# Four gated cross-attention layers on one core: L3's routing moved into the attention before it, half of L2's folding moved into L1's mixture

## The chip, the cores and the metric

The kernel runs on one core of a Trainium2 chip. The core has five engines with instruction streams of their own: TensorE (PE: matmuls and transposes, from SBUF into PSUM), VectorE (DVE), ScalarE (ACT: activation functions through loaded tables, copies), GpSimd (POOL: here mostly powers, some elementwise work, and the issuing of indirect DMAs) and SyncE (SP: issues the other DMAs). They wait for one another through semaphores. The metric is the device time of one execution in microseconds (us); a smaller number is better. All data are float32.

## The reference

The state `x` has 8 sequences of 256 tokens with 128 features (2048 tokens); the context `ctx_2048` has 8 x 64 tokens of 256 features. Four layers, L0 to L3, each add a cross attention and a feed-forward part, both behind a layer norm and scaled by a tanh gate:

```python
for n in range(4):
    x = x + tanh(g_xattn[n]) * Ln_xattn(layernorm(x), ctx_2048, ...)
    x = x + tanh(g_ffn[n])   * Ln_ffn(layernorm(x), ...)
```

The parts are, cut to what matters here:

- `L0_ffn`: a base SwiGLU MLP and the top 2 of 8 SwiGLU experts.
- `L1_xattn`: 16 heads of 8 features; the keys are the layer's own 256 tokens and the 64 context tokens.
- `L1_ffn`: the top 2 of 8 gelu experts (hidden size 64) and a shared expert:

```python
scores = sigmoid(x @ gate_W) * route_scale          # 8 experts
gate_full = top-2 of scores, divided by their sum, zero elsewhere
h = gelu(einsum('bsd,edh->bseh', x, W1) + b1)
out = sum_e gate_full[e] * (h[e] @ W2[e] + b2[e]) + gelu(x @ Ws1 + bs1) @ Ws2 + bs2
```

- `L2_xattn`: 16 heads of 64, keys and values from the context plus one null key and value; the output is layer-normed.

```python
q = x @ Wq;  k, v = split(context @ Wkv)            # 16 heads of 64
k = concat(null_k, k);  v = concat(null_v, v)
out = layernorm(softmax(q k^T / 8) v @ Wout) * ln_scale + ln_bias
```

- `L2_ffn`: an attention whose projections are mixed over 8 experts, and then 8 gelu experts.
- `L3_xattn`: 8 heads of 16 over the masked context tokens, without projections.
- `L3_ffn`: a shared silu expert, and the one expert of 8 with the largest router probability, both with weights quantised to three values a row:

```python
h = layernorm(x) * ln_gamma + ln_beta
probs = softmax(h @ router_w.T)                     # 8 experts
out = shared(h) + max(probs) * expert[argmax(probs)](h)
```

## The kernel before

**Tiling.** `x` stays in SBUF as 16 tiles of 128 tokens. A chunk (`c`, 0 to 3) is 512 tokens, four tiles; a half is two chunks, eight tiles (`HT`). Two large SBUF tiles, `arena_a` and `arena_b`, hold one layer's weights and intermediates after another's; a new use of an arena waits for the old one's readers. PSUM is handed out in banks of 128x512 (`bank`) and pairs of banks (`banks2`). The steps run in the order `l0, l1_xattn, l1_ffn, l2_xattn, l2_ffn, l3_xattn, l3_ffn`.

**What sets the order.** In L0 to L2 a tile scheduler places each engine's instructions from the order of the program and the dependences; `behind(X)` keeps what is issued in it behind instruction X. A tile of a pool may be given memory that another pool's closed tile had; its first writer then waits for that tile's last readers. In L3 (`manual_schedule`) each engine issues in the order of the program.

**L0's end and L1's attention.** L0's feed-forward gathers rows of expert results back to their tokens with indirect DMAs (`gather`, L610) through the index tile `dp_rows`, made in `placed` (L585). L1's attention goes over the eight sequences `bb`: `maxima(bb)` forms scores (`sc`, L983) and their negated maxima (`nmx`, L992); `finish()` turns the maxima with PE (`pm`, L999), copies them (`nmT`, L1001) and sends them by DMA into four rows of the queries (L1003), so that `outputs(bb)` can form exponentials of scores less maximum (`stc` L1022, `st` L1038, `pT` L1047) and sum values (`o`, L1064), divide, turn and project. `prepare(c)` makes chunk c's queries, keys and values ahead, in pieces (`extra`) set among the steps.

**L1's mixture** (`l1_ffn`): `route(0)`, `route(1)` (norm, turn `pt` L272, copy `xT` L1150, logits `lg` L1152, sigmoid L1156, top 2 into `w4`), then `hidden(c)` (five matmuls `ph` L1168 and gelus L1175, L1178) one chunk ahead of `output(c)`: turn the weights (`pg`, `gt` L1188), spread them over hidden rows (`pgb`, L1193), multiply on DVE, and contract (`yt` L1197, L1198, L1200), turn back and add to x. Issue order:

```python
route(0)
route(1)
hg = hidden(0)
for c in range(NCH):
    nxt = hidden(c + 1) if c + 1 < NCH else None
    output(c, hg)
    hg = nxt
```

**L2's folding** (in `l2_xattn`): for each k of 8 pairs of heads, keys and values of the context are formed (`pk` L1374, `pv` L1379) and multiplied into Wq and Wout (`pg` L1395, `pu` L1407), which gives `G` and `U`; scores of L2's attention are then x times G. The null key and value give `gn` (L1363) and `nvu` (L1365). POOL clears `nkb` and two block-diagonal tiles `vds` by memset.

**L3.** `l3_xattn` runs 16 tiles through a software pipeline with a step for each tile; `beside(t, f, ...)` sets work for L3's feed-forward at the end of steps t, t+1, and so on. That is `normed3(c)` (normed x for the attention's queries), `logits3(c)` (stats, norm with z written to DRAM, turn and router logits L1968) and `routed3(half)` (largest logit, counts, positions, and the index list `idx` by which tiles of 128 tokens with one expert each are gathered: 8 + 7 = 15 tiles a half). `l3_ffn` gathers these tiles (`fetched3`: `xr` from z, on POOL, L610), and loops over 30 tiles: `turn`, `first` (L2031, silu), `turn_back` (L2039), `second` (`yr`, L2048, written to DRAM as y). `wide`, `shared`, `back` (L2063, L2070, L2078) are the shared expert of a chunk; `combined(half)` gathers y back by token and adds it. The tail is the gathering for half 1 and the write of the output.

Of the kernel before, what the change touches and what calls it, by code (L numbers as in the profile page):

```python
# [24 lines left out]
P = 128  # L25
# [3 lines left out]
NCH = 4  # L29
# [8 lines left out]
def tile_flamingo(ctx: ExitStack, tc: tile.TileContext, a: dict, out: bass.AP, n_sub: int = 8):  # L38
# [9 lines left out]
    @contextmanager  # L48
    def psum(singles, pairs):

        with ExitStack() as st:
            for n, bufs in ((1, singles), (2, pairs)):
                if not bufs:
                    continue
                ps[n] = st.enter_context(tc.tile_pool(name=f"ps{n}", bufs=bufs, space=bass.MemoryType.PSUM))
            yield
# [458 lines left out]
    def counted(pool, masks):  # L515
# [10 lines left out]
        v.tensor_copy(cnt, pc)  # L526
        return cnt

    def placed(pool, masks, cnt, consts):
# [55 lines left out]
        rows = mk(pool, [P, n_sel, HT], "dp_rows", dtype=I32)  # L585
# [369 lines left out]
    def l1_xattn():  # L955
# [5 lines left out]
        with psum(2, 3), tc.tile_pool(name="l1x", bufs=2) as lp:  # L961
# [140 lines left out]
            before, after = None, []  # L1102
            for bb in range(B):
# [3 lines left out]
                extra = prepare(ahead) if bb % BPC == 0 and ahead < NCH else []  # L1107
                for n in range(5):
# [8 lines left out]
                    for q in (extra, after):  # L1117
                        if q and (q is extra or n > 0):
                            q.pop(0)()
# [9 lines left out]
            before(3)  # L1129
            for f in after:  # L1130
                f()


    def l1_ffn():
        load2()
        with psum(8, 0), tc.tile_pool(name="l1f", bufs=2) as lp:

            e_pair = mk(lp, [P, 4, P], "e_pair", bufs=1)
            for j in range(4):
                r = slice(32 * j, 32 * j + E)  # L1140
                v.tensor_copy(e_pair[r].rearrange("p g (t h) -> p (g t) h", t=2), over(ident[r, r], 64))
            w4 = mk(lp, [P, NT, 4, 32], "w4", bufs=1)
            g.memset(w4, 0.0)
            xT = mk(lp, [P, NCH, CW], "xT", bufs=1)

            def route(half):
                lg = bank([P, HT, E], "lg")
                for k2 in range(2):
                    c = 2 * half + k2
                    s.copy(xT[:, c, :], transposed(layernorm(c)))  # L1150
                    for k in range(TPC):
                        pe.matmul(  # L1152
                            lg[:, k2 * TPC + k, :], xT[:, c, k * P : (k + 1) * P], gw1, start=True, stop=True
                        )
                sc = mk(rt, [P, HT, E], "sm_p")
                s.activation(sc, lg, AF.Sigmoid)  # L1156
# [1039 lines left out]
```

## Time and profile before

| | us |
|---|---|
| median of 3 timed runs (lowest to highest) | 1296.32 (1294.29 to 1307.2) |
| profiled execution, its own time | 1218.13 |
| its span, mean granted clock | 1216.3, 0.909 |
| PE busy, share of span | 1043.9, 86% |
| DVE, ACT, POOL busy | 640.1, 442.5, 304.9 |
| L1's attention, from its first scores to the last values | 231 to 491 |
| L1's mixture | 491 to 576 |
| L2's folding | 576 to 639.5 |
| L2's attention and feed-forward | 639.5 to 1056 |
| L3's attention | 1056 to 1129 |
| L3's feed-forward up to the last `yr` | 1129 to 1198 |
| tail | 1198 to 1216.3 |

The stages are read from the timeline's times, and overlap a little. Times on the page are from the span's start. The "granted clock" is the share of full speed that the throttle gave PE. A line of the timeline has start, length, engine, line, operation and operands, and, in brackets, the engine's idle time just before it and what ended it. The chain of waits is followed back from the last instruction, at each step to what released it.

### The profile page before, as it was taken

Reading aid. Unit: us, or ns where it says so; the run is one execution under the profiler, and the core shown is the slowest. Engines: PE = TensorE matmul, PEld = TensorE weight load, DVE = VectorE, ACT = ScalarE, POOL = GpSimd, SP = SyncE. Lnnn points to the kernel's source line nnn. Section 1 sums busy time; section 2 is a strip of 40 time slices with the busy share of each in tenths; the row PEclk is TensorE's granted clock in tenths of the full one; section 3 lists DMA queues with packets and bytes.
Section 4 is the critical chain, followed back from the end, with each engine's and each line's share of the span. In section 5 each row is a group of like instructions: output and inputs, shape, how many; then the busy total and the mean of one; then the engine's idle time right before and its main releaser. Section 6 shows DMA issues by size and latency. Waiting matters only on the chain.

```text
span 1216.3 us, 15651 instructions
## 1 busy us (share of the span) xinstructions
PE 1043.9 (86%) x5570; PEld 580.8 (48%) x5570; DVE 640.1 (53%) x1776; ACT 442.5 (36%) x860; POOL 304.9 (25%) x341
## 2 busy tenths in 40 slices
PE   5889998848999899898998987879998989875894
PEld 4548756624444444533555654334433333343573
DVE  4574536535555454534237996454463733487353
ACT  3623433313344345422234444122102443364442
POOL 2137541221000000101102555122231410132554
PEclk9889999858999999788898997889989999997798
DMA  9203310200000012300000000200000000000233
GB/s 241 68 20 57 76 46 19 58 24 20 3 20 2 19 42 65 104 0 1 1 1 1 1 1 9 78 1 0 1 1 1 0 1 1 0 10 9 50 70 98
DMA packets 50811, 37.04 MB, mean 30 GB/s; under 512 B 10280, under 2 KB 46672, under 8 KB 50480
## 3 DMA queue, kind: packets, MB, share of 16 engines
q1 hardware_dynamic: 45488, 26.83, 8.0%
q0 software_dynamic: 3968, 8.13, 3.7%
q10 hardware_dynamic: 1280, 1.09, 0.5%
q8 instruction: 45, 0.74, 0.3%
q14 instruction: 30, 0.25, 0.1%
HBM read 25.34 MB, written 8.13 MB: 28 GB/s over the span
## 4 chain that ended last, share of the span: by engine, by line
PE 65%; DVE 16%; ACT 6%; issue 5%; POOL 5%; DMA 1%; SPq 0%; POOLq 0%; DVEq 0%; ACTq 0%
PE pymT L1610 5%; PE st L1038 4%; PE gur L768 3%; PE o L1064 3%; PE pqmT L1610 3%; DVE nmx L992 3%; PE sc L983 3%; PE phm L1693 2%; PE pgb L1591 2%; PE pvmT L1610 2%; PE pkmT L1610 2%; PE yr L793 2%; PE yt L1200 2%; PE gu L744 2%; POOL xn L610 1%
## 5 line engine op out<-in xcount | busy, mean ns | idle before, releaser
L992 DVE TENSOR_REDUCE nmx<-sc 128x2 f32<-128x640 f32 x128 | 97.5, 818 | 64.1 <-PE sc L983 63.0
L221 POOL TENSOR_TENSOR rstd<-rstd,mhalf 128x4 f32<-128x4 f32 (+1 forms) x36 | 34.2, 949 | 343.3 <-DVE rstd L236 296.4
L1047 ACT ACTIVATE pT<-st 128x1024 f32<-128x1024 f32 x64 | 62.1, 1021 | 104.6 <-PE st L1038 104.6
L768 PE MATMUL gur<-arena_a,xrT 128*128 x184 | 63.6, 471 | 0.4
L1610 PE MATMUL pymT<-xe,arena_b 128*128 128x512 f32 x128 | 61.7, 638 | 2.6 <-DVE xe L1602 2.6
L610 POOL DMA_INDIRECT xr<-xk,dp_src x46 | 46.8, 1017 | 43.3 <-DVE lg_m L289 29.7
L1464 POOL TENSOR_TENSOR arena_a<-arena_a,rs 128x1024 f32<-128x1024 f32 x16 | 30.4, 1901 | 92.6 <-DVE rs L1463 77.9
L1591 PE MATMUL pgb<-gt,e_sel 8*128 8x512 f32 x192 | 40.4, 704 | 7.6 <-ACT gt L1584 7.6
L983 PE MATMUL sc<-arena_b 29*128 29x320 f32 x256 | 41.1, 553 | 4.7 <-DVE nmx L992 4.0
L785 DVE COPY aTr<-pta 128x256 f32<-128x256 f32 x46 | 19.5, 424 | 47.6 <-PE pta L783 47.5
L1610 PEld LDWEIGHTS pymT<-xe,arena_b 128*128 128x128 f32 x128 | 25.4, 204 | 38.6 <-issue 23.7
L610 POOL DMA_INDIRECT xn<-yg,dp_rows x32 | 30.4, 950 | 41.9 <-issue 32.1
L983 PE MATMUL sc<-arena_a 29*128 29x320 f32 x256 | 35.8, 472 | 4.2 <-DVE nmx L992 3.9
L277 DVE SCALAR_TENSOR_TENSOR x<-yt,tg,x 128x512 f32<-128x512 f32 x16 | 11.9, 748 | 51.5 <-PE yt L1205 25.7
L768 PEld LDWEIGHTS gur<-arena_a,xrT 128*128 128x128 f32 x184 | 32.2, 193 | 13.5 <-issue 2.1
L793 PE MATMUL yr<-arena_a,aTr 128*128 (+1 forms) x276 | 38.3, 276 | 0.0
L1443 PE MATMUL sc<-G,t2k 128*128 128x512 f32 x64 | 34.3, 633 | 4.6 <-DVE rs L1462 3.7
L1940 POOL TENSOR_TENSOR arena_a<-arena_a 128x256 f32<-128x256 f32 x18 | 13.6, 757 | 91.0 <-DVE arena_a L1939 90.5
L610 POOL DMA_INDIRECT xr<-z,dp_src x30 | 28.5, 951 | 30.0 <-DVE rstd L1953 14.7
L776 ACT ACTIVATE sgr<-gur 128x352 f32<-128x352 f32 x46 | 21.4, 465 | 39.5 <-PE gur L768 39.5
L1038 PE MATMUL st<-arena_b 32*128 32x256 f32 x256 | 34.6, 466 | 1.3 <-DVE nmx L992 1.0
L1610 PE MATMUL pqmT<-xe,arena_b 128*128 128x512 f32 x64 | 35.1, 711 | 0.0
(505 smaller groups left out, 2400.6 us busy)
## 6 DMA issues: line engine op xcount, KB each, us to landing
arena_a<-in_L_ffn_exp_wgu_dram SPq DMA_DIRECT2D x2, 1408.0 KB
yg<-yr SPq DMA_DIRECT2D x10, 256.0 KB
arena_a<-in_L_xattn_Wkv_dram SPq DMA_DIRECT2D x1, 2048.0 KB
y<-yr SPq DMA_DIRECT2D x6, 256.0 KB
x<-in_x_dram SPq DMA_DIRECT2D x4, 256.0 KB
arena_b<-in_ctx_dram ACTq DMA_DIRECT2D x2, 512.0 KB
arena_a<-in_L_ffn_exp_wd_dram SPq DMA_DIRECT2D x2, 512.0 KB
xk<-xk SPq DMA_DIRECT2D x4, 256.0 KB
```

The costliest lines, as they stand in the source:

```text
L221: g.tensor_tensor(dst, src, mhalf[:, 0:n], ALU.pow)
L610: return g.indirect_dma_start(out=dst, out_offset=None, in_=src, in_offset=bass.IndirectOffsetOnAxis(ap=idx, axis=0))
L768: pe.matmul(gu[:, h, 0:352], xrT[t], wgu[:, bass.ds(e + 1, 1), h * 352 : h * 352 + 352].rearrange("p e f -> p (e f)"), start=True, stop=True,)
L793: pe.matmul(y, aT[0:n, i, :], wd[0:n, bass.ds(e + 1, 1), i, :].rearrange("p e d -> p (e d)"), start=(i == 0), stop=(i == 2),)
L983: pe.matmul(scs[j // 2][:, j % 2, 0:K], qp[i : i + 29, k4, t], kp[i : i + 29, k4, b, :], start=True, stop=True,)
L992: l1["max"] = v.tensor_reduce(nmx[qt][:, h0 : h0 + 2], scs[pr][:, :, 0:K], AX.X, ALU.max, negate=True)
L1038: pe.matmul(sts[j // 2][:, j % 2, kt, :], kp[i : i + 32, k4, b, kt * P : (kt + 1) * P], qp[i : i + 32, k4, tb], start=True, stop=True,)
L1047: s.activation(pT[k4, pr], sts[pr], AF.Exp)
L1064: pe.matmul(o[kk][32 * i : 32 * i + n, k, :], w, e, start=(step == 0), stop=(step == 2))
L1443: pe.matmul(sc[:, 8 * k : 8 * k + 8, :].rearrange("p h m -> p (h m)"), xT[:, q], G[:, b, 8 * k : 8 * k + 8, :].rearrange("p h m -> p (h m) ...
L1591: pe.matmul(pg, e_sel4[r, e, :], gt[r], start=True, stop=True)
L1610: pe.matmul(pq, w[:, e, :], xe[:, e, :], start=(e == 0), stop=(e == E - 1))
```

## The change

The change has three groups; the words that came with it name the second and third.

1. `placed` takes the tile `dp_rows` from the constant pool, with two buffers for each count of selections, instead of from the pool of the step that calls it. It serves L0 and L3.
2. `l1_ffn` and `l2_xattn` become one step, `l1_l2`, in one PSUM layout. Chunk 0's norm and logits (`route1(0)`), and the expander `e_pair`, are set into the last two sequences of L1's attention, and `hidden1(0)` before its last divide. Sigmoid becomes 1/(1+exp(-x)) on raw logits. Four of the eight foldings of L2 are placed among the outputs of the mixture; the null key and value, L2's constants and the load of L2's feed-forward weights (`load2`) come behind it. `w4` and `vds` are cleared by ACT copies instead of POOL memsets; the spread weights are multiplied in pairs of banks. Pieces of `prepare` are put behind the latest maximum. `G` and `U` become two tiles each.
3. In L3's attention the steps that prepare the feed-forward come a step earlier, the turn and the logits are steps of their own, half 0's whole routing lies in steps 11 to 15 and its gathers begin at step 15. The exponential and the probability of the routed expert (`weighed3`) are taken out of the routing. In L3's feed-forward the expert tiles come first; logits of chunks 2 and 3, routing of half 1 and the shared expert of chunks 0 to 2 lie among them.

```diff
@@ placed @@
-        rows = mk(pool, [P, n_sel, HT], "dp_rows", dtype=I32)
+        rows = mk(const, [P, n_sel, HT], f"dp_rows{n_sel}", bufs=2, dtype=I32)
...
@@ l1_xattn @@
-        with psum(2, 3), tc.tile_pool(name="l1x", bufs=2) as lp:
+        with psum(2, 3, True), tc.tile_pool(name="l1x", bufs=2) as lp:
...
+            asides = {6: [lambda: None, l1_arena], 7: route1(0, misc)}
...
-                extra = prepare(ahead) if bb % BPC == 0 and ahead < NCH else []
+                extra = prepare(ahead) if bb % BPC == 0 and ahead < NCH else asides.get(bb, [])
...
-                            q.pop(0)()
+                            with behind(l1["max"]) if q is extra else ExitStack():
+                                q.pop(0)()
...
             before(3)
+            hidden1(0, l1["hg0"])
             for f in after:
                 f()
...
@@ l1_ffn @@
-            w4 = mk(lp, [P, NT, 4, 32], "w4", bufs=1)
-            g.memset(w4, 0.0)
+        w4 = mk(lp, [P, NT, 4, 32], "w4", bufs=1)
+        clear(w4.rearrange("p n j e -> p (n j e)"))
...
-                s.activation(sc, lg, AF.Sigmoid)
-                v.tensor_scalar(sc, sc, rscale, None, ALU.mult)
+            s.activation(sc, es[:, h, :], AF.Exp, scale=-1.0)
+            v.tensor_scalar(sc, sc, 1.0, None, ALU.add)
+            v.reciprocal(sc, sc)
+            v.tensor_scalar(sc, sc, rscale, None, ALU.mult)
...
+        steps = [route1(c, misc) for c in range(1, NCH)]
+        for norm, logits in steps[:1]:
+            norm()
+            logits()
+        hidden(1)
+        for norm, logits in steps[1:]:
+            norm()
+            logits()
+        routed(0)
+        hidden(2)
+        fold()
+        with behind(l1["ph"]):
+            output(0)
+        fold()
+        routed(1)
+        hidden(3)
+        output(1)
+        fold()
+        output(2)
+        fold()
+        output(3)
+        fold()
...
@@ l2_xattn, now in l1_l2 @@
-            for t in vds:
-                g.memset(t, 0.0)
...
+            def folds():
...
+                with behind(l1["ph"]):
+                    kv = keys_values(0)
+                yield
                 for k in range(8):
+                    nxt = keys_values(k + 1) if k < 7 else None
+                    fold(k, *kv)
+                    kv = nxt
+                    yield
...
+            for t in vds:
+                for b4 in range(2):
+                    clear(t[:, 4 * b4 : 4 * b4 + 4].rearrange("p b t m -> p (b t m)"))
+            pieces = folds()
+            with tc.tile_pool(name="l1f", bufs=2) as lp:
+                l1_ffn(lp, misc, lambda: next(pieces))
+            late_tiles(r2["pool"], 0)
+            load2()
+            with tc.tile_pool(name="l2c", bufs=1) as cp, tc.tile_pool(name="l2x", bufs=2) as lp:
+                half_tiles(cp)
+                constants2()
+                run_all(pieces)
+                l2_xattn(lp)
...
@@ l3_xattn @@
-            beside(3, *normed3(2))
-            beside(7, *normed3(3))
+            beside(2, *normed3(2))
+            beside(6, *normed3(3))
             for c in range(2):
-                beside(4 * c + 5, *logits3(c))
+                beside(4 * c + 4, *logits3(c))
             steps = routed3(0)
-            beside(12, *[lambda: next(steps, None)] * 5)
-            beside(13, *logits3(2))
+            beside(11, *[lambda: next(steps, None)] * 5)
+            n_tiles = HT + E - 1
+            beside(15, lambda: fetched3(0, range(4)))
+            q3["late"] = logits3(2), logits3(3)
+            beside(15, *q3["late"][0][0:2])
+            beside(16, lambda: (q3["late"][1][0](), fetched3(0, range(4, n_tiles))))
...
@@ logits3, routed3 @@
-        return [stats, norm, logits]
+        return [stats, norm, turn, logits]
...
-        s.activation(pr, pr, AF.Exp)
...
+    def weighed3(half):
+
+        pr = q3["pr", half]
+        s.activation(pr, pr, AF.Exp)
+        q3["w", half] = w = mk(q3["pool"], [P, HT], "w3")
+        row_sum(w, pr)
+        v.reciprocal(w, w)
+        v.tensor_scalar(w, w, tg[:, 7:8], None, ALU.mult)
...
@@ l3_ffn @@
+            weighed3(0)
+            turn2, logits2 = q3["late"][0][2:]
+            norm3, turn3, logits3_ = q3["late"][1][1:]
+            norm3()
+            turn2()
+            beside(-2, logits2, turn3, logits3_)
+            beside(1, *[lambda: next(steps, None)] * 5)
+            aside[6] = [lambda: fetched3(1, range(n_tiles))]
...
+            for i in range(3):
+                shared_beside(7 + 3 * i, i)
+            aside[n_tiles].append(lambda: backs.extend(combined(0)))
...
+            weighed3(1)
             h3 = wide(3)
             tail = combined(1)
             y3 = shared(3, h3)
+            backs[0]()
+            backs[1]()
             back(3, y3)
```

`clear(dst)` is an ACT copy of zeros, used before in L1's preparation; `shared_beside(t, c)` sets `wide(c)`, `shared(c)` and `back(c)` at tiles t, t+1 and t+2.

## The prediction

> **What bounds the kernel now.** I read the page first, to see which engine carries the end; then the table of windows, cut at the stages, to see where that engine is not working at full speed; then the timeline and the chain of waits inside the stages that the diff touches.
>
> ```profile
> PEclk9889999858999999788898997889989999997798
> PE 65%; DVE 16%; ACT 6%; issue 5%; POOL 5%; DMA 1%; SPq 0%; POOLq 0%; DVEq 0%; ACTq 0%
> ```
>
> The second line is the chain that ended last: TensorE (PE) has 65% of it. The first is the granted clock in 40 slices of 30.4 us, in tenths: it is not full in most. So what can be won is time in which PE waits, and PE work done at less than full clock. The columns of the next lines are window, its length, busy us and instructions of PE, PE weight loads, VectorE (DVE), ScalarE (ACT) and GpSimd (POOL), then PE clock, DMA share and GB/s.
>
> ```profile
> 490.00:523.00 33.00, 27.58 (x112) 16.55 (x104) 18.35 (x68) 15.54 (x23) 4.92 (x5) 0.74 0.30 96
> 523.00:582.00 59.00, 51.01 (x129) 19.26 (x128) 21.85 (x73) 13.91 (x21) 7.93 (x7) 0.86 0.00 0
> 582.00:640.00 58.00, 56.46 (x256) 33.48 (x257) 18.08 (x32) 18.57 (x33) 0.00 (x0) 0.94 0.00 1
> 1070.00:1125.00 55.00, 36.12 (x180) 20.88 (x178) 43.03 (x136) 29.57 (x65) 16.77 (x17) 0.82 0.03 10
> 1125.00:1170.00 45.00, 38.98 (x192) 28.51 (x193) 19.57 (x77) 20.55 (x45) 23.02 (x25) 0.80 0.27 55
> 1170.00:1200.00 30.00, 28.90 (x187) 23.36 (x185) 16.36 (x48) 15.66 (x40) 14.11 (x15) 1.00 0.49 103
> ```
>
> L1's mixture (490 to 582) and the start of L2's folding run at clock 0.74 to 0.94, with PE idle for 15 of the first 150 us. L3's attention (1070 to 1125) has PE busy 36 of 55 us; the start of L3's FFN (1125 to 1170) has clock 0.80.
>
> **Part C, the rows tile (not in the change's words).** `dp_rows` moves from L0's pool to the constant pool. In the timeline:
>
> ```profile
> 244.21 0.38 PE L999 MATMUL pm<-ident,nmx 128*16 128x128 f32 x1
> 256.62 0.41 DVE L1001 COPY nmT<-pm 16x256 f32<-16x256 f32 x1 [11.47 <-DMA xn<-yg,dp_rows]
> ```
>
> The first copy `nmT` of L1's attention has its input at 244.6, but waits until 256.6 for the last gathers of L0: its tile lies where `dp_rows` lay, and they still read it. Behind it stand the DMA of 2.19 us that brings nmT to the queries, and the first `stc` matmul (258.84, after 13.25 us without PE). With the rows elsewhere, the copy waits for `pm` alone. The transpose pair ends near 245, plus a semaphore: the copy goes at about 245.7, **-10.9 us**. What is late next are the same gathers for the chunks of half 1, which the attention first needs near 261, while they land at 256: no new wait once shifted, unless these steps come up to 3 us early. Ends: -8 and -11.5.
>
> **Part A, the mixture with half of the folding in it.** I add up the PE work from the attention's last values (490.9) to the last fold (639.5), at full clock, from these steps of the chain:
>
> ```profile
> 507.60 3.41 PE ph L1168 x4
> 531.17 3.44 PE ph L1168 x8
> 596.78 1.72 PE pk L1374 x4
> 598.50 1.72 PE pv L1379 x4
> 600.22 1.06 PE pg L1395 x4
> 601.27 1.98 PE pu L1407 x16
> ```
>
> The first two show the clock: the same shape takes 3.41 us for four records at half clock and 3.44 for eight at full. A hidden chunk is 3.44 + 0.86 (one more tile, a quarter of 3.44) = 4.3, four 17.2. An output is 3.44 (w2a) + 1.9 (ws2, b2a) + 1.1 (pgb) + 0.9 (eight transposes) = 7.4, four 29.5. Routing is 0.45 + 0.96 a chunk, 5.6. A fold is 1.72 + 1.72 + 1.06 + 1.98 = 6.48, eight 51.8. The attention's tail is 2.7; gn and nvu took 6.9 at clock 0.5 to 0.6, so 3.6. Sum **110**, where 148.6 pass: 38 us are idle or half clock.
>
> After, chunk 0's routing (1.4) goes into the attention's last steps. There PE is busy 19.45 of 20 us, so it is paid there: +1.4. The rest has two phases. In the first (tail, three hidden chunks, routing of chunks 1 to 3, first `pk`: 2.7 + 12.9 + 4.2 + 1.7 = 21.5 us of PE) ACT has more to do than PE. It now also clears w4 and two `vds` tiles, which POOL's memsets did: 4 copies of 128x512 at 0.59 (the row of xT's copy) and one of 128x2048 at some 1.9 (0.59 continued by 0.43 for each further 512). Fifteen gelus at 0.69 are 10.3, the other copies 2.8, logits and exps 1.4, clears 4.3, and **seven table loads** (gelu, exp, gelu, sigmoid for L2's constants, gelu, exp, gelu; four before in this stretch, where the sigmoid comes later).
>
> ```profile
> 513.69 1.28 ACT L1156 ACT_TABLE_LOAD   x1
> 514.98 0.22 ACT L1156 ACTIVATE sm_p<-lg 128x64 f32<-128x64 f32 x1
> ```
>
> By this row a load is 1.28 us and the next activation starts at once: seven are 9.0, ACT's sum is 27.8. [...] the gelu before ends at 513.67, the load starts at 513.69. I take the row.
>
> The second weighing is the clock. [...] phase one, [...] is ACT's: it ends at 491 + 28 = 519. In the trace half clock set in at 494, after gaps of 0.3 to 1.4 us, and in the slice 506 to 510 it was still 0.50, though PE had been busy without a gap since 501.3; it rose only at about 510.8. By the row all PE work behind the first hidden chunk can run at half, 2 x 15 us, ending near 527. I take 523, between the two.
>
> From 523 PE has 110 - 1.4 - 21.5 = 87 us left. Four folds now lie between the outputs' steps, so a chain pg, gt copy, pgb, multiply, yt has folds beside it where before PE stood or dropped to half (538 to 546, 566 to 574, 582 to 590). The stretch 590 to 640, folds alone, holds 1.00. I allow 4 us of stalls: end 523 + 87 + 4 + 1.4 = 615.5 against 639.5, **-24**. Ends: phase one to 531 and 8 us of stalls, -12; phase one to 519 and none, -32.
>
> Edits with one answer: `Wkv` is issued at 490.5 as before and needed at about 518 (landed near 501). L2's FFN weights are issued on SP's queue after the mixture rather than ahead of it, needed near 762: no cost, 180 us of cover. DVE's pair multiplies, prepare's statistics behind the maxima and the exp form of the sigmoid cost DVE under 1 us each, with DVE at a third of this stretch.
>
> **Part B, L3.** In the attention:
>
> ```profile
> 1090.77 0.42 DVE L1849 TENSOR_TENSOR on<-po,rs 128x256 f32<-128x256 f32 x1 [3.23 <-PE po L1845]
> 1108.78 0.42 DVE L1849 TENSOR_TENSOR on<-po,rs 128x256 f32<-128x256 f32 x1 [6.02 <-PE po L1845]
> 1133.42 1.05 POOL L610 DMA_INDIRECT xr<-z,dp_src  x1 [14.69 <-DVE rstd L1953]
> ```
>
> In the first two DVE stands still 3.2 and 6.0 us: PE is held at its router logits, which wait in one step for z's transposes and ACT's turn. Split over two steps most of that goes: about -7.5, less a new wait of 1.3 at step 11, where `largest` follows the logits in its own step: -6. Routing starts a step (3.4 us) earlier, and its last parts, which stood after the attention, lie in it. So the indices are ready near 1121.5 rather than 1133, and the 15 gathers on POOL (a pace of 1.25 us, done at 1152 before) begin there; ahead of them on POOL stand only the norms' powers (0.95 each), behind them those of chunk 3, up to 5 us late and not urgent. The tile loop starts with half 0's expert tiles near 1130 instead of 1146, but the three shared chunks that filled the wait move into it. From 1130, 30 tiles at 1.21 (phr to phr), three shared chunks of 3.9, logits 2.8 and counts and indices 2.4 are 53.3 us: 1183.5. Half clock at the start and routing of half 1 among the first tiles cost some 7: the last `yr` at 1190.5 instead of 1198, **-7.5**. Ends: -3 (no more than the attention's stalls, half given back) and -14 (no stall).
>
> The tail is unchanged, with eight gathers, their landing and the output:
>
> ```profile
> 1209.90 2.52 DMA xn<-y,dp_rows
> ```
>
> `weighed3(1)`, the two late `backs` and back(3) now stand there too, some 8 us of ACT and DVE beside eight gathers at 1.25 on POOL. If that cover fails, up to 3 us.
>
> **Sum.** -10.9 - 24 - 7.5 = **-42.4**. The profiled execution took 1218.1 us (span 1216.3), so it would be 1175.7. The timed median is 1296.3, 6% above, for a reason that the profile cannot show: taking off 42.4 gives 1253.9, and the ratio 0.965 gives 1251.2. I say **1252 us**.
>
> **Rivals.**
>
> - *ScalarE keeps the mixture.* [...] the gelus, now in line behind clears and table switches, leave PE sparse: phase one ends near 532, A is -15, and B only its low end, -3: about -29, **1267**. For it: 28 us of ACT in some 32. [...]
> - *All warm.* No half clock in the merged stretch and none in the tile loop: -11.5 - 32 - 14 = -57.5, **1237**. For it: 1.00 from 590 on and in 1170 to 1200. Against: L3's start at 0.80 although busy.
> - *Half clock holds in the interleaved stretch: slower.* Each us of work done at half clock adds one. The gains are used up when 42 of the 87 us behind phase one run so; at 61 (70%) the sum is +19, **1315**. For it: three stretches with PE busy nearly throughout and clock 0.50 to 0.66. Against: those followed waits for one output chain, and folds alone ran at 1.00.
> - *The change doesn't do what it says in L3:* the indices are early, but first expert tiles wait for rows still in gathering, and the loop ends as before. B is 0: -35, **1261**.
>
> **How the numbers follow.** Forecast (-30 to -52) 0.58, ScalarE 0.20, all warm 0.10, L3 empty 0.06, half clock 0.06. A change of 1%, 13 us, is about what a measurement of this kernel can tell from none (the runs before spread by as much). Half clock is split evenly between slower and within; one hundredth of ScalarE falls within. So faster 0.93, same 0.04, slower 0.03. The range takes the low ends of all parts (-23) to near the all-warm sum scaled by 6% (-61), rounded outward: 1232 to 1276.
>
> **What would show it.** Right: nmT's copy straight behind `pm` and PE without a hole of 13 us near 245; the last fold 24 us nearer to the attention's end, clock near 1.00 after the third hidden chunk; the first xr gather before the last `po` of L3's attention, and the last yr 7 us nearer to it. Wrong: [...] clock 0.5 between the folds; PE waiting on xr in the first tiles. The forecast fails if the merged stretch is not at least 12 us shorter.

## The result, and the profile after

The changed kernel takes 1286.57 us (median of 20 runs, 1280.71 to 1297.66) where the kernel before, beside it, takes 1303.12 (1292.11 to 1311.91). The ratio over the runs is **0.9898**, interval 0.9868 to 0.9927, so some 13 us faster (the two medians alone are 16.6 apart). The forecast was -42 us, at 1252 us. The direction holds, the size does not: about a third of it was there, and the time lies outside the range given.

One thing has to be known to read absolute times. The chips that ran these kernels are of two kinds: on chips 1, 3 and 7 the kernel before takes about 1225 us, on chip 10, and beside the result above, about 1300. The changed kernel moves with it (1205 and 1287). By its time the profile of before comes from the first kind, and the one taken with the result above from the second. On the second kind engines stand with their inputs ready in L0's tile loop while POOL issues gathers, as in these two lines of its timeline (their inputs were written by 119.2 and 122.9):

```profile
129.24 0.27 ACT L767 COPY xrT<-ptr 128x128 f32<-128x128 f32 x1 [7.01 <-remote]
137.64 0.42 DVE L790 COPY aTr<-pta 128x256 f32<-128x256 f32 x1 [10.21 <-remote]
```

So kernels are compared on one chip alone, and the stages are read below from a run of the changed kernel on a chip of the first kind (`e13_after_third`: 1204.92 us, ratio 0.983, interval 0.9779 to 0.9881). Its clock and chain:

```profile
PEclk9888999859999999998999987988999999986698
PE 66%; DVE 15%; ACT 7%; POOL 4%; issue 3%; DMA 3%; SPq 1%; POOLq 0%; DVEq 0%; ACTq 0%
```

And its windows, at the stages of those shown before (columns as there):

```profile
486.00:519.00 33.00, 26.80 (x110) 12.71 (x106) 14.72 (x64) 27.43 (x41) 2.37 (x4) 1.00 0.30 96
519.00:578.00 59.00, 57.28 (x188) 24.55 (x180) 24.63 (x59) 14.38 (x24) 3.02 (x3) 0.91 0.00 1
578.00:619.00 41.00, 40.26 (x186) 23.20 (x187) 14.85 (x33) 12.28 (x22) 3.91 (x2) 0.96 0.30 77
1049.00:1104.00 55.00, 34.31 (x176) 20.83 (x176) 43.52 (x117) 27.66 (x60) 16.31 (x16) 0.82 0.03 10
1104.00:1149.00 45.00, 31.90 (x151) 25.59 (x152) 18.76 (x79) 15.34 (x36) 21.28 (x22) 0.65 0.22 46
1149.00:1185.00 36.00, 36.00 (x228) 28.73 (x227) 17.96 (x47) 20.56 (x52) 17.17 (x19) 1.00 0.36 78
```

The mixture's first 33 us are ACT's now (27.43 busy), at full clock; the next 59 have PE busy 57. That part works. The attention of L3 (1049 to 1104) is nearly as before. The stretch behind it (1104 to 1149) is worse: PE busy 31.9 of 45 us where it was 39.0, clock 0.65 where it was 0.80.

The stages by trace, in us, from landmarks in each timeline: `st` and `po` are products of the attentions of L1 and L3, `pu` closes a fold, `pbt` is the last product of L2, `xr` a gather, `phr` and `yr` are the first and the last product of an expert tile. The kernel before is shown by `e2_rows_only`, which has the rows tile alone of the change:

| stage | `e2_rows_only` | changed (`e13_after_third`) |
|---|---|---|
| L1: last st to last pu (mixture, folding) | 154.4 | 134.6 |
| L3: L2's last pbt to the last po | 73.8 | 75.0 |
| last po to the first xr gather | 3.7 | -1.8 |
| last po to the first phr of the tile loop | 17.6 | 11.9 |
| first phr to the last yr | 50.5 | 63.1 |
| last yr to the end | 18.3 | 18.9 |

The first row is 151.4 in the profile of before, from which the forecast was made, and 154.4 in those of `e1_before_again` and `e4_rows_l3` too.

### The profile page after: what moved, and what is told of

It is laid out like the page before. It is cut to its first block, busy times and chain, and to the rows that moved or that the text cites. A ratio compares the mean times of both kernels' runs of the same rounds, so it can differ in the third digit from the quotient of the medians.

```text
span 1285.2 us, 15646 instructions
## 1 busy us (share of the span) xinstructions
PE 1063.9 (83%) x5570; PEld 591.4 (46%) x5570; DVE 639.3 (50%) x1762; ACT 451.5 (35%) x875; POOL 299.9 (23%) x338
## 4 chain that ended last, share of the span: by engine, by line
PE 64%; DVE 15%; ACT 7%; issue 6%; POOL 4%; another core or an unknown queue 3%; DMA 1%; SPq 1%; POOLq 0%; DVEq 0%; ACTq 0%
PE pymT L1678 5%; PE sc L988 4%; PE gur L773 4%; PE st L1043 4%; PE o L1069 3%; DVE nmx L997 3%; PE pqmT L1678 3%; PE phm L1761 2%; PE pgb L1659 2%; PE pvmT L1678 2%; PE pkmT L1678 2%; PE yr L798 2%; PE yt L1226 2%; PE gu L749 2%
## 5 line engine op out<-in xcount | busy, mean ns | idle before, releaser
L773 PE MATMUL gur<-arena_a,xrT 128*128 x184 | 69.7, 507 | 0.3
L988 PE MATMUL sc<-arena_b 29*128 29x320 f32 x256 | 43.7, 563 | 10.7 <-issue 5.2
L1518 POOL TENSOR_TENSOR arena_a<-arena_a,rs 128x1024 f32<-128x1024 f32 x16 | 30.4, 1902 | 58.7 <-DVE rs L1517 44.3
L788 PE MATMUL pta<-ident,sgr 128*128 128x128 f32 x138 | 24.6, 289 | 21.3 <-DVE sgr L782 11.9
L773 PEld LDWEIGHTS gur<-arena_a,xrT 128*128 128x128 f32 x184 | 34.8, 209 | 16.2 <-issue 6.7
L798 PE MATMUL yr<-arena_a,aTr 128*128 (+1 forms) x276 | 41.0, 288 | 0.0
L798 PEld LDWEIGHTS yr<-arena_a,aTr 128*128 128x128 f32 (+1 forms) x276 | 37.0, 203 | 0.5 <-issue 0.2
L2116 DVE COPY h1T<-pth 128x256 f32<-128x256 f32 x30 | 12.7, 423 | 46.1 <-PE pth L2114 27.8
```

The source lines that it names most:

```text
L773: pe.matmul(gu[:, h, 0:352], xrT[t], wgu[:, bass.ds(e + 1, 1), h * 352 : h * 352 + 352].rearrange("p e f -> p (e f)"), start=True, stop=True,)
L798: pe.matmul(y, aT[0:n, i, :], wd[0:n, bass.ds(e + 1, 1), i, :].rearrange("p e d -> p (e d)"), start=(i == 0), stop=(i == 2),)
L988: pe.matmul(scs[j // 2][:, j % 2, 0:K], qp[i : i + 29, k4, t], kp[i : i + 29, k4, b, :], start=True, stop=True,)
```

## The experiments

### The parts apart

**`e1_before_again`** is the kernel before, unchanged.

> The kernel before, unchanged, profiled once more. Theory 1 (the profiled execution of before, 1218 us, was not a usual one): the time is about 1300 us, and L0's and L3's expert tile loops carry the difference: L0's last gur ends near 265 to 275 us rather than 226, with PE, ACT and DVE standing several us at a time while POOL issues gathers, as in the profile of after. Then the -42 of the prediction has to be looked for between two usual executions. Rival (the change itself slows L0 and L3): about 1218 us again, last gur at 226, and the stalls are the change's.

Measured: 1231.06 us (one run), the last `gur` (the first product of L0's expert tiles) at 228.6, with before at 1226.95 beside it. Theory 1 fell as it was put: the profiled execution of before was no odd one, it came from another kind of chip than the timed runs. The rival's blame of the change fell too, since before itself takes 1300 us on a chip where the changed kernel takes 1287.

**`e2_rows_only`**: part C alone.

```diff
-        rows = mk(pool, [P, n_sel, HT], "dp_rows", dtype=I32)
+        rows = mk(const, [P, n_sel, HT], f"dp_rows{n_sel}", bufs=2, dtype=I32)
```

> Part C alone: the rows tile from the constant pool, all else as before. By the prediction -10.9 us (-8 to -11.5): the first nmT copy straight behind its transposes. Theory 1: between 0 and -11, since in a usual execution the gathers of L0 may end at another time against the maxima, so that the wait is not 11 us. Rival: slower by up to 45 us, if the place of the tile is what makes L0's loop slow.

Measured: 1214.45 us against 1226.95, ratio 0.9906 (0.9877 to 0.9935), so -11.5 us. In its timeline the copy follows its transposes at once; the 11.47 us of waiting in front of it have become 0.48:

```profile
245.40 0.38 PE L999 MATMUL pm<-ident,nmx 128*16 128x128 f32 x1 [0.61 <-DVE nmx L992]
245.82 0.41 DVE L1001 COPY nmT<-pm 16x256 f32<-16x256 f32 x1 [0.48 <-PE pm L999]
```

**`e3_rows_mixture`**: the changed kernel with the L3 of before (parts C and A).

```diff
@@ l3_xattn, logits3, routed3, l3_ffn @@
-            beside(2, *normed3(2))
...
+            beside(3, *normed3(2))
...
```

> Parts C and A (rows, mixture with folding), L3 as before. By the prediction -35 us. By the profile of after, where the stretch from the attention's last st to the last fold is 134.6 us against 151.4 in the profile of before: A is about -17, so C and A together -17 to -28.

Measured: 1196.96 us, ratio 0.9792 (0.9745 to 0.9839). Against `e2_rows_only` that is -17.5 us for A; the stretch from the last st to the last pu takes 136.3 us against 154.4, -18.2.

**`e4_rows_l3`**: the kernel before with the rows and the new L3 (parts C and B).

```diff
@@ l3_xattn, logits3, routed3, l3_ffn @@
-            beside(3, *normed3(2))
...
+            beside(2, *normed3(2))
...
```

> Parts C and B (rows, L3's new order), mixture and folding as before. By the prediction -18 us. Theory of a loss in L3: the gathers, now issued while the expert tiles and the attention run, hold the other engines up, the loop takes 102 us from the first gather to the last yr instead of 64, and B gives back all of C and more: +5 to +30 us against C alone. Rival (the loop is as slow in a usual execution of before): B is -3 to -8, the sum -5 to -18.

Measured: 1226.8 us, ratio 1.0008 (0.9981 to 1.0035): all of C is given back. Against `e2_rows_only` B costs 12 us by the medians; in the traces L3, from L2's last pbt to the end, takes 168.2 us against 160.2, so **+8**. The rest does not lie in L3: from the first nmT to the last st of L1's attention, where both kernels have the same code, the two traces take 241.6 and 239.1 us, and two traces of the kernel before take 230.7 and 237.5. B is the part that failed.

### L3's start

These four ran on chip 10, of the second kind (before 1300.35 us). **`e5_after_again`** is the changed kernel.

> The changed kernel, unchanged, beside the others. If the parts add up, C and A (-30 us in e3_rows_mixture) plus B (e4_rows_l3 less e2_rows_only, +12 us) give about -18 us, a ratio near 0.985, and in its profile L0's last gur ends near 225 us and L3 takes from the last po to the last yr some 75 us (68 in the profile of before). If the parts hinder one another, the ratio is nearer to 0.99.

Measured: 1287.71 us, ratio 0.9914 (0.989 to 0.9937), L0's last gur at 270.9: the kind of chip, not the change, decided about L0. L3 takes 194.0 us here.

**`e6_norm_first`**:

```diff
-            beside(15, lambda: fetched3(0, range(4)))
             q3["late"] = logits3(2), logits3(3)
-            beside(15, *q3["late"][0][0:2])
+            beside(14, q3["late"][0][0])
+            beside(15, lambda: fetched3(0, range(4)))
+            beside(16, q3["late"][0][1])
```

> The changed kernel with chunk 2's statistics one step earlier (14), so that POOL forms their power ahead of the first four gathers, not behind them; the norm at step 16 as before. Theory 1 (PE stands behind turn2, which waits for that power: 4.9 us at 1136 to 1141 in e4_rows_l3; DVE, in order, holds chunk 3's statistics behind it too, and POOL's eleven gathers behind those): 3 to 5 us faster than e5_after_again. Rival (the loop is bound by the gathers' pace and the half clock, not by turn2): within 1 us of e5_after_again.

Measured: ratio 0.9902 (0.9872 to 0.9933), which can't be told from `e5_after_again` by the times. In the trace the first phr comes 3.1 us earlier behind the first gather, and L3 takes 190.2 us, -3.8. What it removes is seen in the changed kernel's timeline (`e13_after_third`):

```profile
1112.26 0.94 POOL L615 DMA_INDIRECT xr<-z,dp_src  x1 [0.30 <-issue]
1113.23 1.05 POOL L222 TENSOR_TENSOR rstd<-rstd,mhalf 128x4 f32<-128x4 f32 x1
1114.31 0.16 DVE L359 SCALAR_TENSOR_TENSOR nm<-mv,rstd 128x4 f32<-128x4 f32 x1 [3.17 <-POOL rstd L222]
1115.06 1.64 PE L273 MATMUL pt<-ident,xn 128*128 128x128 f32 x4 [4.92 <-ACT xn L361]
1117.62 1.02 POOL L615 DMA_INDIRECT xr<-z,dp_src  x1 [0.18 <-issue]
```

Chunk 2's power stands behind four gathers on POOL; DVE waits 3.2 us for it, PE 4.9 at the turn of chunk 2, which lies ahead of the first tile; and since chunk 3's statistics are behind it on DVE, POOL stands too before gather five, from 1113.2 on but for two powers. Three engines, each issuing in the order of the program, wait for one instruction of 1 us.

**`e7_cover`**:

```diff
+            h0, h1 = wide(0), wide(1)
             norm3()
+            y0 = shared(0, h0)
+            y1 = shared(1, h1)
             turn2()
+            back(0, y0)
+            back(1, y1)
...
-            for i in range(3):
-                shared_beside(7 + 3 * i, i)
+            shared_beside(n_tiles - 4, 2)
...
```

> The changed kernel with the shared expert of chunks 0 and 1 ahead of the tile loop again, as before the change; routing and gathers as in the changed kernel. Theory 1 (the gathers' latency and the norms need cover, and PE work taken from there and put into the loop is paid in full): some 7.8 us at full clock leave the loop and fill a stretch in which PE was busy 4 of 12 us: 5 to 9 us faster than e5_after_again. Rival (the loop has slack, since it waits for gathers and routing): no faster, within 2 us.

Measured: ratio 0.9898 (0.986 to 0.9937), again not to be told from `e5_after_again` by the times; in the trace L3 takes 189.2 us, -4.8, with the loop at 81.7 instead of 88.5 and its start 2.2 later. That is just under the lower edge of what theory 1 said.

**`e8_idx_late`**:

```diff
-            beside(11, *[lambda: next(steps, None)] * 5)
+            beside(11, *[lambda: next(steps, None)] * 4)
+            beside(16, lambda: next(steps, None))
...
-            beside(15, lambda: fetched3(0, range(4)))
...
-            beside(15, *q3["late"][0][0:2])
+            beside(14, *q3["late"][0][0:2])
+            beside(16, lambda: fetched3(0, range(4)))
```

> The changed kernel with the last part of half 0's routing (dp_idx and what leads to it) at step 16, behind the attention's last outputs, and with it the gathers; chunk 2's statistics and norm at 14 and 15. Theory 1 (in the attention this part is not free: dp_idx takes 3.6 us on PE at half clock after a wait of 1.3 us ahead of the last o, and DVE's part lies ahead of the last softmax): the last po comes 4 to 6 us earlier after L2, the first gather at most 2 us later, and the whole is 0 to 4 us faster. Rival (an early start of the gathers is what counts): slower by 1 to 4 us.

Measured: ratio 0.993 (0.9892 to 0.9967). The attention takes 74.94 us, the same as with the index product in it (74.97). That does not refute theory 1, for the edit also sets chunk 2's statistics and norm a step earlier, and the norm took the product's place. The last `o` of the attention was there at 1166.4, 4.1 us earlier behind the last pbt than in the changed kernel, where the index product holds it up; but ACT had the norm ahead of its copy `oT`:

```profile
1165.36 1.08 PE L1905 MATMUL o<-pT,vc 128*32 128x256 f32 x8 [0.68 <-ACT pT L1899]
1169.12 1.65 ACT L361 ACTIVATE xn<-x,nm,rstd 128x128 f32<-128x128 f32 x4 [3.81 <-DVE nm L359]
1170.67 0.35 ACT L1907 COPY oT<-o 128x256 f32<-128x256 f32 x1
```

So what the index product costs in the attention stays open. The first gather comes 5.5 us later, and L3 takes 193.7 us, as in `e5_after_again`. But chunk 2's power goes ahead of the gathers here, as in `e6_norm_first`, and beside that run (190.2) L3 is 3.5 us longer and the first phr comes 5.4 later. An early first gather is thus worth something once the power is out of its way; how much is not shown, since the norm's step differs too (15 here, 16 there).

### Back on chips of the first kind

**`e9_rows_mixture_again`** is the kernel of `e3_rows_mixture`.

> Parts C and A without B again (the kernel of e3_rows_mixture), as the base of the next two and for the price of B beside the changed kernel. Theory 1 (B costs 8 to 12 us): ratio to before 0.976 to 0.982, against 0.985 to 0.991 for all three parts. Rival (C and A gain less than the six runs of e3_rows_mixture said, and B costs nothing): a ratio near 0.99.

Measured: 1197.36 us, ratio 0.978 (0.9727 to 0.9833). C and A together are confirmed, at -27 us.

**`e10_lean_clears`**:

```diff
-        clear(w4.rearrange("p n j e -> p (n j e)"))
+        g.memset(w4, 0.0)
...
-                for b4 in range(2):
-                    clear(t[:, 4 * b4 : 4 * b4 + 4].rearrange("p b t m -> p (b t m)"))
+                g.memset(t, 0.0)
```

> As e9_rows_mixture_again, but w4 and the two vds tiles are cleared by POOL's memsets, as before the change, and not by ACT's copies. Theory 1 (the first phase of the mixture is ACT's, 27.8 us of it, 4.3 us of which are clears): the stretch from the attention's last st to the last fold is 3 to 5 us shorter. Rival (that phase is paced by the round trip of PE, PSUM and the table loads, and the clears fall in gaps of ACT): less than 1 us.

Measured: 1193.51 us, ratio 0.9763 (0.971 to 0.9815); the interval does not part it from `e9_rows_mixture_again`. In the trace the stretch takes 128.3 us against 134.5, -6.2: more than the 4.3 us of copies. 3.2 come before the first pu, which is phase one; 3.0 behind it, where two output products (yt) that had run at half clock now run at full (3.70 us each). Other runs repeat it: with ACT's clears the stretch takes 133.6 to 136.3 us in ten traces, with POOL's 128.3, 129.9 and 129.9 (here, in `e11_lean_shared` and in `e15_all_edits`). So the first phase does wait for ACT, by 3.2 of the 4.3 us; why the clock held for more of the products behind it was not settled.

**`e11_lean_shared`**:

```diff
-            aside[n_tiles - 4] = [lambda: mid.update(h=wide(2))]
-            aside[n_tiles - 3] = [lambda: mid.update(y=shared(2, mid["h"]))]
-            aside[n_tiles - 2] = [lambda: back(2, mid["y"])]
+            aside[1].append(lambda: mid.update(h=wide(2)))
+            aside[2].append(lambda: mid.update(y=shared(2, mid["h"])))
+            aside[3].append(lambda: back(2, mid["y"]))
```

> As e10_lean_clears, and in L3's tile loop the shared expert of chunk 2 lies at tiles 1 to 3, among half 1's routing, not at tiles 11 to 13. Theory 1 (where PE waits for the routing's VectorE steps, work of the shared expert costs nothing: PE is busy 6 of 8 us there at clock 0.79): L3 from the first phr to the last yr 2 to 4 us shorter than in e10_lean_clears. Rival (the dp_idx wait is behind the same engine's gathers and moves with them): within 0.5 us.

Measured: 1192.99 us, ratio 0.9734 (0.968 to 0.9789). From the first phr to the last yr 47.1 us against 50.6, -3.4, of which the tail gives 1.0 back. So most of a shared chunk (3.9 us in the prediction's sum) is free in the loop where PE waits for routing.

**`e12_norm_cover`** has the edits of `e6_norm_first` and `e7_cover`.

> The changed kernel with both edits of e6_norm_first (chunk 2's statistics ahead of the gathers) and e7_cover (shared chunks 0 and 1 ahead of the tile loop). Theory 1 (the two losses of L3's start add: POOL's order and missing cover): L3 from L2's last pbt to the end 6 to 9 us shorter than in the changed kernel (168 us in e4_rows_l3 where before takes 162; 194 in e5_after_again), so no slower than L3 before. Rival (they are one loss, since both end when the gathers do): 4 to 5 us shorter.

Measured: 1198.15 us, ratio 0.9793 (0.9729 to 0.9857). L3 takes **157.4 us** against 168.2 in `e4_rows_l3`, -10.8, and 3 less than L3 before (160.2): the two losses add, and a little more than theory 1 said. The times do not show the 3 us: the ratio is 0.978 in `e9_rows_mixture_again`, which has the L3 of before. The start of L3's FFN in its timeline:

```profile
1108.54 1.01 POOL L222 TENSOR_TENSOR rstd<-rstd,mhalf 128x4 f32<-128x4 f32 x1 [5.03 <-DVE rstd L2026]
1110.73 1.05 POOL L615 DMA_INDIRECT xr<-z,dp_src  x1 [1.19 <-DVE rs L1915]
1113.00 5.90 PE L2139 MATMUL ph<-xT,bq_w 128*128 128x512 f32 x8 [0.52 <-DVE on L1917]
```

The power now goes ahead of the first gather, and PE has the shared expert from 1113.0 on, 0.5 us behind the attention. The whole window up to the loop:

```profile
1112.50:1125.00 12.50, 12.00 (x40) 6.52 (x41) 4.37 (x15) 9.15 (x19) 9.72 (x11) 0.80 0.40 90
```

PE is busy 12.0 of 12.5 us. In the changed kernel (`e13_after_third`) it was busy 3.95 of 12:

```profile
1110.00:1122.00 12.00, 3.95 (x15) 2.81 (x15) 2.96 (x14) 4.37 (x11) 8.12 (x9) 0.50 0.28 78
```

**`e13_after_third`** is the changed kernel on a chip of the first kind.

> The changed kernel once more, on a chip where before takes about 1225 us if this is one: C + A (-27 us) and B (+8 us in the trace of L3) give -19 us, ratio 0.983 to 0.987. Rival (B's price depends on what runs ahead of it, and is less in the whole change): 0.980 or below.

Measured: 1204.92 us, ratio 0.983 (0.9779 to 0.9881), L3 168.8 us. The parts add up: -27 and +8 give -19, which the interval (-14.6 to -27) holds.

**`e14_norm_step`** is `e12_norm_cover` with one more edit:

```diff
-            beside(2, *normed3(2))
-            beside(6, *normed3(3))
+            beside(3, *normed3(2))
+            beside(7, *normed3(3))
```

> As e12_norm_cover, with the norms of chunks 2 and 3 for the attention at steps 4 and 8 again, as before the change, and not at 3 and 7. Theory 1 (four activations of a norm, 1.65 us, set at the end of an odd step, stand on ScalarE right ahead of the next even step's oT copy, for which po and then VectorE's on wait, 1.2 to 1.6 us each of four times; so the two long stalls of before came back as short ones): two of the four waits go, and the attention from L2's last pbt to the last po takes 72 to 73 us instead of 75. Rival (VectorE is the bound there, and a stall that goes is only filled by the next wait): within 0.5 us of 75.

Measured: 1196.96 us, ratio 0.9782 (0.9724 to 0.984). The attention takes 73.4 us, -1.6: between the two. Two of the short waits go, but those left grow, 2.5, 1.9 and 2.9 us where they were 1.4, 1.2 and 2.0. And the tile loop takes 54.6 us instead of 51.8. One window at the same place in it shows where, first of `e12_norm_cover`, then of `e14_norm_step`:

```profile
1141.00:1149.00 8.00, 8.00 (x50) 7.29 (x50) 3.04 (x9) 3.72 (x10) 5.00 (x6) 0.79 0.23 52
```

```profile
1135.00:1143.00 8.00, 8.00 (x34) 7.37 (x34) 2.00 (x8) 1.76 (x5) 3.77 (x4) 0.50 0.09 22
```

PE is busy all of the 8 us in both, but at half clock it gets 34 matmuls done and not 50. `e15_all_edits` has the same window at 0.50 and a loop of 54.6 us too. Why the clock fell for longer there was not settled.

**`e15_all_edits`** is `e14_norm_step` with the clears of `e10_lean_clears`.

> As e14_norm_step, and w4 and vds cleared by POOL's memsets (e10_lean_clears). If the edits add up: e12_norm_cover less 6 us for the clears less what e14_norm_step gains, a ratio of 0.970 to 0.974, and the fastest of all. Rival (the clears' gain hides behind another wait here): 0.976 to 0.979.

Measured: 1193.7 us, ratio **0.9726** (0.9673 to 0.9779), the smallest of all. Its six runs, up to 1196.09, all lie below the six of the changed kernel beside it, from 1199.58. The ratio is what was expected if the edits add up, but not all of them did: the clears' gain is there (129.9 us instead of 136.2 from the last st to the last pu), that of `e14_norm_step` is not (L3 takes 159.4 us, and took 157.4 in `e12_norm_cover`). `e11_lean_shared` (0.9734) is not to be told from it.

## Why the prediction was wrong, point by point

In the forecast's own terms, beside what was measured on chips of the first kind:

| part | forecast, us | measured, us | the step that failed |
|---|---|---|---|
| C, rows | -10.9 | -11.5 | none here; on the second kind see below |
| A, mixture | -24 | -17.5 | 4 us of stalls were 8.8, and 87 us of PE work 94 |
| B, L3 | -7.5 | +8 (traces) | the attention, -6, became +1.2; the loop's start, 6.3 us behind the last po, became 11.9; the loop, 60.5, became 63.1 |

The forecast of -42.4, less 15.5 for B and 6.5 for A, and with 0.6 more for C, is the -21 of `e13_after_third` (ratio 0.983).

**Part C was right** on these chips, by the mechanism named, although the change's own words do not mention it. On the second kind, where the result was taken, the gain was probably not there. In the profile of that run the last gather of L0 is issued at 298.28, and its last packet has landed at 300.5, while the maxima are ready only at 304.1:

```profile
298.28 0.94 POOL L615 DMA_INDIRECT xn<-yg,dp_rows  x1 [0.30 <-issue]
304.12 0.38 PE L1004 MATMUL pm<-ident,nmx 128*16 128x128 f32 x1 [6.02 <-DVE nmx L997]
304.54 0.41 DVE L1006 COPY nmT<-pm 16x256 f32<-16x256 f32 x1
```

A copy at 304.5 has no gather left to wait for, wherever its tile lies. This fits the smaller net there (13 us, and 21 in `e13_after_third`), but is not shown, since the kernel before was not profiled on that kind. The step that failed is then the transfer: a wait read in an execution of 1218 us was taken off runs of 1296 us, without knowing what made the 6% between them.

**Part A had the right mechanism and two terms too small.** Forecast -24; the stretch from the last st to the last pu became 15 to 20 us shorter, -17.5 by the times. Phase one was right: ACT's sum was put at 27.8 us, to end 28 us behind the attention's last values, and the first `pk` ended 28.6 us behind them (486.6 to 515.2), with ACT busy for 25.6. The clears put at 0.59 and some 1.9 us took 0.62 and 1.90 (the 0.43 for each further 512 columns is what `pT`'s 1.02 us at 128x1024 has over 0.59 in the profile of before). The row of 1.28 us for a table load held: there are seven loads, each of 1.28 us, with ACT idle for 0.02 us or less on either side of each, as in these lines of its timeline:

```profile
508.57 1.28 ACT L1200 ACT_TABLE_LOAD   x1
509.86 0.26 ACT L1200 ACTIVATE sm_p<-pbias 128x64 f32<-128x64 f32 x1
510.14 1.28 ACT L1183 ACT_TABLE_LOAD   x1
```

For the clock I had taken a middle (32 us, to 523) between ACT's 28 us (to 519), which took PE to be at full clock, an assumption of mine that no trace of before showed, and the row at 494 to 510 (to 527). The first was the better choice for phase one, which ran at 1.00 although PE stood idle for 1.6 to 2.2 us three times. Behind it three products of four fell to half clock for a part of their time, with PE idle for only 0.4 to 0.7 us beside them, which is nearer to the row at 494, where the gaps ahead were of 0.3 to 1.4 us.

What failed lies behind phase one. From the end of the first `pk` at 515.2 to the last pu at 617.6 pass 102.5 us, where 87 + 4 were forecast. Summed over windows of 0.4 us, PE is idle for 2.2 of them and loses 6.6 to half clock: 8.8 us, where "I allow 4 us of stalls". The other 93.7 us are PE work at full clock, 7 more than the sum of 87 had. The half clock shows in the chain of waits:

```profile
521.21 5.38 PE yt L1226 x8
542.26 1.23 DVE hg L1221
543.54 3.70 PE yt L1226 x8
558.13 1.23 DVE hg L1221
559.40 6.76 PE yt L1226 x8
578.39 5.40 PE yt L1226 x8
```

Three of four output products run partly at half clock (5.38, 6.76 and 5.40 instead of 3.70). DVE's multiply of the second pair, 1.23 us, stands open on the chain at each output (the two shown, and one ahead of each of the other products); the folds lie between the outputs, but not between this multiply and its product. PE has one small product beside it and is idle for only 0.4 to 0.7 us of it. Why the clock falls there was not settled.

**Part B had the wrong sign**: -7.5 forecast, +8.0 in the traces (+12 by the medians of `e4_rows_l3` and `e2_rows_only`). The 15.5 us between forecast and traces are 7.2 in the attention, 5.6 at the loop's start and 2.6 in the loop.

First, "split over two steps most of that goes: -6". The attention became 1.2 us longer. DVE's waits did not go, they were spread:

```profile
1055.00 0.42 DVE L1917 TENSOR_TENSOR on<-po,rs 128x256 f32<-128x256 f32 x1 [1.63 <-PE po L1913]
1063.74 0.42 DVE L1917 TENSOR_TENSOR on<-po,rs 128x256 f32<-128x256 f32 x1 [1.38 <-PE po L1913]
1072.57 0.42 DVE L1917 TENSOR_TENSOR on<-po,rs 128x256 f32<-128x256 f32 x1 [1.46 <-PE po L1913]
1081.10 0.42 DVE L1917 TENSOR_TENSOR on<-po,rs 128x256 f32<-128x256 f32 x1 [1.16 <-PE po L1913]
1085.66 0.22 DVE L290 TENSOR_REDUCE lg_m<-lg 128x8 f32<-128x64 f32 x1 [1.71 <-ACT lg L2043]
1091.65 0.42 DVE L1917 TENSOR_TENSOR on<-po,rs 128x256 f32<-128x256 f32 x1 [2.04 <-PE po L1913]
```

These six are 9.4 us, and 2.4 more come at the index product; before had 3.2 + 6.0, and 4.0 at its very last `on`. The first four follow a norm, four activations of 1.65 us in all, which ACT now has at the end of odd steps, right ahead of the copy `oT` that the even step's `po` needs. `e14_norm_step` moved two of these norms and got 1.6 us: the cause is a part of it, the rest is filled by the next wait. The new wait of 1.3 us that I had seen is the one at `lg_m`, with 1.7. DVE's routing work moved ahead of the last po adds to that: from the last pbt to the last po DVE is busy 58.8 us where it was 55.8, and idle 16.2 where it was 18.0. I had counted this work as lying in the attention at no cost, with DVE busy 43 of 55 us in front of me.

Second, "the tile loop starts near 1130", which is 6.3 us behind the last po of the forecast. The gathers began 5.5 us earlier against the last po, about as forecast (the rest of the 12 us was to be the attention's). But I wrote that the norms' powers stand ahead of them on POOL. The order written in the step is the other way round: four gathers, then chunk 2's power, and the loop's first tile behind chunk 2's turn on PE. `e6_norm_first` gives the price, 3.8 us.

Third, the shared expert was counted as work that only changes its place. Its 11.7 us were in the loop's sum (chunk 2's lay in the loop before, so that two chunks had filled the wait, not three). But the 7.8 us of those two had been the cover of the gathers' latency: without them the loop began 11.9 us behind the last po, with PE idle for two thirds of that time. `e7_cover` gives 4.8 us back, and both edits together 10.8.

Fourth, half clock: the first 24 us of the loop ran at 0.65 to 0.79 (the first 24 us of the loop of `e2_rows_only` at 0.79 to 1.00). Summed over windows of 0.4 us, the loop's 63.1 us are 52.3 of PE work at full clock, 4.1 idle and 6.6 lost to half clock; in the profile of before 44.3, 4.5 and 1.7. So the 53.3 us of work in the sum were right, and the 7 us allowed for the rest were 10.7. In `e12_norm_cover` the loop is 45.4, 4.7 and 1.7: with the shared expert ahead of it again the half clock went too. That the one keeps the clock up for the other is not shown apart.

The tail moved by less than 1 us, as forecast, and so did L2 (from the last pu to the last pbt). **The rivals:** the total came nearest to "ScalarE keeps the mixture" (-29), but by luck and not by its mechanism, for A was at -15 to -20, and phase one ended 28.6 us behind the attention's last values, where that rival had 41 (491 to 532). "Half clock holds in the interleaved stretch" was there in small, 7 us of the 42 that it needed. None of the rivals had L3 lose: I had asked of each moved step what waits for it, but not what had been hidden behind the work that was moved away.

## What to carry to other kernels

Work that looks movable may be the cover of a latency; before it is taken out, look at what the engine would do in its place, and put it back where PE waits, not where PE is busy (the shared expert of two chunks cost 4.8 us in the wrong place, and most of a third's was free among the routing). Where engines issue in the order of the program, an early bulk of DMA issues must go behind the small instruction that the next stage waits for: four gathers of 1.25 us ahead of one power of 1 us held three engines. A part of a change that its words leave out, one tile's pool, gave 11.5 us where the whole change gave 21. And when a profile and the timed runs of one kernel differ by 6%, a wait seen in the one may not be there in the others.

## What the runs showed of the hardware

Two kinds of chips ran the same program in about 1225 us (chips 1, 3 and 7) and 1300 us (chip 10). Each chip was used at one time only, so that it is the chip, and not something else of that time, is not shown. On the slower kind the stretches in which POOL issues gathers carry the difference: L0's expert tiles, from the first gur to the last, take 183 to 187 us instead of 138 to 143, from there to the first nmT 32 to 33 us pass instead of 18 to 20 (rows tile moved), and L3's loop in the changed kernel takes 88 instead of 63. ACT, DVE and PE stand for up to 10 us with inputs ready there, while gathers are issued at the same pace of 1.25 us as on the other kind. The mean clock of the profiled executions differs little (0.88 to 0.89 against 0.89 to 0.92). What holds the engines was not found; the kernel before was not profiled on such a chip.

A loaded table cost ACT 1.28 us and no more, in seven loads of the changed mixture (488 to 512 us in `e13_after_third`), with 0.02 us or less of idle ACT before and after each. The length of PE's idle time did not tell whether the clock falls: three gaps of 1.6 to 2.2 us left it at 1.00 (502 to 513 us in `e13_after_third`), and beside gaps of 0.4 to 0.7 us it fell (the output products from 521, 559 and 578 us on took 5.38, 6.76 and 5.40 us and not 3.70). Nor is it the same each time: in two profiles of the kernel before, the part of L1's attention from 420 to 480 us ran at 1.00 in one (`before`) and at 0.78 to 0.90 in the other (`e1_before_again`). From the first nmT to the last st these two took 230.7 and 237.5 us, which is 6.8 of the 12.9 us by which their spans differ.
